# A graph network on one core: the convolutions' second parts one step later, and one scratch write fewer behind the gathers

## The chip, the cores and the metric

The kernel runs on one core of a Trainium2 chip. A core has five engines with queues of their own: TensorE multiplies matrices into PSUM, VectorE and ScalarE work element by element, GpSimd issues the gathers here, and SyncE issues plain transfers. The metric is the time of one execution on the device in microseconds. Three runs of the kernel before took 7125.32, 7131.07 and 7133.75 us; the median is 7131.07 us.

## The reference

There are 6250 nodes with 128 features and 200000 edges, sorted by destination. The function is a layer norm with a ReLU, two mesh convolutions with a group norm and a Silu behind each, and an attention over the edges; the parts are added up at the end. The change touches the convolutions only:

```python
def mesh_conv(x, src, dst, ea, w1, b1, g, bt, w2, b2):
    m = jnp.concatenate([x[dst], x[src], ea], axis=-1) @ w1 + b1
    m = jax.nn.silu(group_norm(m, g, bt))      # 8 groups of 16, per edge
    m = m @ w2 + b2
    out = jax.ops.segment_sum(m, dst, num_segments=n)
    cnt = jax.ops.segment_sum(jnp.ones((dst.shape[0],), m.dtype), dst, num_segments=n)
    return out / jnp.clip(cnt, 1.0)[:, None]
```

## The kernel before, in words

The edges are cut into 196 chunks of 1024 (`NCH` chunks, `NT` = 8 columns of 128 edges). A convolution multiplies by `w1` at the nodes and not at the edges: the part of the destination lies in the table `a_d`, the part of the source in `b_d`. Since the edges are sorted, a chunk needs a short run of 112 rows of `a_d`, which SyncE loads (L606), and a matmul with a one-hot matrix (`ohT`, made by ScalarE on L615 and L616 from loaded offsets) spreads them over the edges (L1000, tile `m`). The rows of `b_d` are gathered by GpSimd, eight indirect transfers of 128 rows to a chunk (`gather`, L622), into one of four buffers `g`. Behind a chunk's eight gathers GpSimd writes zeros into a scratch tile that nobody reads (L634), `REST` times: three times in the convolutions, four times in the attention. The next chunk's gathers stand behind these writes on GpSimd's queue.

A chunk's work in a convolution has two parts. The first part adds the gathered rows to `m` (L1006, VectorE, into one of four buffers `h`), squares the sum (L1008, ScalarE) and reduces it to one sum of squares for each edge and group (L1009, VectorE, tile `var`). Two chunks make a run: for a run ScalarE takes one square root (L1016, tile `sd`) and VectorE one reciprocal of it (L1093), into a PSUM tile that both chunks read. The second part makes the one-hot matrix of the destinations (L639), adds the sums of an earlier chunk to the node table (L1041), normalises with three VectorE passes (L1020, L1023, L1024), applies Silu (L1025, ScalarE), and sums over the edges by matmuls (L1030, TensorE, tile `u`). ScalarE then copies the sums of the chunk before out of PSUM, masked for two windows of 128 nodes (L1036).

`pipeline` writes all of this in steps. In step n a chunk two ahead is fetched (its loads and gathers are issued), the products of the next chunk are computed, the root of a run that is complete is taken (`root`), the one-hot offsets of the chunk two ahead are turned into ones and zeros, then come the second parts that fall due (`second`) and the first part of chunk n. `steps_of` says which second parts fall due in which step: those of a run are spread over the steps up to the end of the next run, and `lag` says how many steps behind the run's end they begin. In the kernel before, `lag` is 0 in the convolutions: in the step that takes the root, the run's first chunk has its second part, so chunk c has its second part in step c + 2. `in_order` pins the written order on VectorE, SyncE, ScalarE and TensorE; GpSimd's order follows from the gathers, each chunk behind the scratch writes of the chunk before.

From step 81 on, batches of four windows whose edges are all summed are processed as nodes between the steps (`conv_nodes`, 14 batches per convolution): a matmul with `w2`, the group norm, whose root is taken with that of a run, and the tables of the next stage. `plan_batches` finds from `steps_of` which chunks are done by then.

Of the kernel before, what the change touches and what calls it, by code (L numbers as in the profile page):

```python
# [24 lines left out]
HD = 16  # L25
NT = 8
CH = NT * P
REST = {1: 3, 2: 3, 3: 4}
G = 8
GC = 2  # L30
BN = 4
# [14 lines left out]
def kernel(ctx: ExitStack, tc: tile.TileContext, x, src, dst, eat, w, out):  # L46
# [280 lines left out]
    def spread(i):  # L327

        sizes, n = ([2, 4, 6], G) if i == 3 else ([1, 1], GC)
        rest, out = NCH, []  # L330
        while rest:
            out.insert(0, min(rest, sizes.pop(0) if sizes else n))
            rest -= out[0]
        return out

    def steps_of(i):


        ends, n, lag = {}, 0, int(i == 3)
        for m in spread(i):  # L340
            ends[n + m] = list(range(n, n + m))
            n += m
        waiting, todo = [], []
        for n in range(NCH + 1 + lag):
            waiting += ends.get(n - lag, ())
            steps = min([m + lag for m in ends if m + lag > n], default=n + 1) - n
            k = -(-len(waiting) // steps)
            todo.append(waiting[:k])
            waiting = waiting[k:]
        return ends, todo  # L350

    def plan_batches(i):

        ends, todo = steps_of(i)
        out, done = [], 0
        for n, now in enumerate(todo):
            done += len(now)
            if n % 8 == (4 if i == 3 else 1) and n > (40 if i == 3 else 80) and n + 6 < NCH \
                    and (i == 3 or n + 5 in ends):
                out.append((n, max(done - 3, 0)))  # L360
        return out if NWD else []
# [258 lines left out]
    def gather(k, g, table_d, rest=0):  # L620
        def start(t):
            return nc.gpsimd.indirect_dma_start(  # L622
                out=g[:, t, :table_d.shape[1]], out_offset=None, in_=table_d,
                in_offset=bass.IndirectOffsetOnAxis(ap=k.src[:, t:t + 1], axis=0))

        with ExitStack() as es:
            if rested and rest:
                es.enter_context(tc.issue_after(rested.pop().ins))
            for t in range(NT):
                last = start(t)  # L630
        if rest:
            with tc.issue_after(last.ins):
                for _ in range(rest):
                    last = nc.gpsimd.memset(nst2, 0.0)  # L634
                rested.append(last)

    def onehot(k, pools, iota):
        k.oh = pools["oh"].tile([P, NT, P], FP, name="oh")
        return nc.vector.tensor_tensor(  # L639
            k.oh, iota[:, None, :].to_broadcast([P, NT, P]),  # L640
            k.dm[:, :, None].to_broadcast([P, NT, P]), ALU.is_equal)
# [71 lines left out]
    def pipeline(i, stage, aside=iter(())):  # L713
# [5 lines left out]

        start = len(nc.cur_bb.bb.instructions)  # L720
        ends, todo = steps_of(i)
        starts = {n: j for j, (n, _) in enumerate(plans[i])}
        ahead = stage.ahead
# [240 lines left out]
    def conv(i):  # L964
# [4 lines left out]
        with ExitStack() as es:  # L969
# [49 lines left out]
            def normed(k):  # L1019
                nc.vector.tensor_tensor(  # L1020
                    k.mt.rearrange("p t (g c) -> p t g c", c=HD), k.mt.rearrange("p t (g c) -> p t g c", c=HD),
                    k.rs.rearrange("p (t g) -> p t g", g=H)[:, :, :, None].to_broadcast([P, NT, H, HD]), ALU.mult)
                nc.vector.tensor_tensor(k.mt, k.mt, over_edges(gam), ALU.mult)  # L1023
                nc.vector.tensor_tensor(k.mt, k.mt, over_edges(bet), ALU.add)  # L1024
                nc.scalar.activation(k.mt, k.mt, AF.Silu)  # L1025

            def summed(k):
                k.u = ps_.tile([P, PITCH], FP, name="u", tag="u", bufs=2)
                for t in range(NT):
                    nc.tensor.matmul(k.u[:, :wide], lhsT=k.oh[:, t, :], rhs=k.h[:, t, :wide],  # L1030
                                     start=(t == 0), stop=(t == NT - 1))

            def by_window(k):
                k.uw = up.tile([P, 2, PITCH], FP, name="uw")
                for q in range(2):
                    nc.scalar.activation(k.uw[:, q, :wide], k.u[:, :wide], AF.Copy,  # L1036
                                         scale=mask[:, q, k.c:k.c + 1])

            def add_late(k):
                s = U[:, bass.ds(value(w0_i, k.c, DVE, NW - 1), 2), :wide]  # L1040
                nc.vector.tensor_tensor(s, s, k.uw[:, :, :wide], ALU.add)  # L1041

            class Stage:
# [4 lines left out]
                def fetch(self, c):  # L1048
                    k = loads(c, pools, a_d[i], self.ahead)
                    k.g = gp.tile([P, NT, D], FP, name="g")  # L1050
                    gather(k, k.g, b_d[i], REST[i])
                    k.h = hs[c % len(hs)]
# [17 lines left out]
                        self.j = 0  # L1070

                def second(self, run, ks):
                    for n, k in enumerate(ks):


                        onehot(k, pools, iota)
                        if self.late:
                            add_late(self.late.pop(0))
                        if n == 0:
                            self.inverse(run)  # L1080
                        normed(k)
                        summed(k)
                        if self.sums:
                            by_window(self.sums[0])
                            self.late.append(self.sums.pop())
                        self.sums.append(k)
                    if not ks:
                        self.inverse(run)

                def inverse(self, run):  # L1090
                    if run:
# [68 lines left out]
    with ExitStack() as es:  # L1160
# [134 lines left out]
        class Stage:  # L1295
# [4 lines left out]
            def __init__(self, bp):  # L1300
                self.bp = bp
                self.runs = list(steps_of(3)[0].values())
                self.nb = load_runs(self.runs.pop(0), bp)

            def fetch(self, c):
                k = loads(c, pools, a_d[3], self.ahead)
                k.g = gp.tile([P, NT, KV], FP, name="g")
                gather(k, k.g, kv_d, REST[3])
                k.qe = []
# [142 lines left out]
```

## Time and profile before

| what | value |
| --- | --- |
| median of three runs | 7131.07 us |
| the profiled execution's own time | 7126.42 us |
| its span, first to last instruction | 7124.6 us |
| GpSimd busy | 5394.0 us (76%) |
| VectorE busy | 5144.2 us (72%) |
| TensorE matmuls busy | 3891.3 us (55%) |
| ScalarE busy | 3308.5 us (46%) |
| gathers of the convolutions | 3136, the first at 56.0 us, the last at 4615.8 us |
| gathers of the attention | 1568, from 4669.4 to 7050.1 us |
| granted TensorE clock, mean | 0.723 |

The span has three stages: the first convolution up to about 2300 us, the second up to about 4640 us, and the attention. In the lines of the profile, POOL is GpSimd, DVE is VectorE, ACT is ScalarE, PE is TensorE and SP is SyncE; `g<-b_d` means that tile `g` is written from `b_d`. A gather's row on POOL is the time in which GpSimd writes its transfer descriptors; the data lands later. Idle time that ended with nothing that the profile shows is called "issue".

### The profile page before, as it was taken

The numbers are of one execution on the slowest core, as the hardware profiler recorded it, in microseconds if no ns is written. First come the engines' busy times: TensorE is split into PE (matmuls) and PEld (weight loads), VectorE is DVE, ScalarE is ACT, GpSimd is POOL, SyncE is SP. The second block draws the span as 40 slices with busy tenths as digits, with TensorE's granted clock in tenths as the row PEclk, the third lists the DMA queues.
The fourth block names the chain that finished last, engine by engine and source line by source line (L and its number), as shares of the span: only waits on it lengthen the run. The fifth ranks groups of instructions, "written<-read, shape, count | busy, mean of one in ns | idle before, by whom it ended". The sixth has DMA issues, their size and how long they took to land. (4 is left out here: it accounts for less than half of the span.)

```text
span 7124.6 us, 74065 instructions
## 1 busy us (share of the span) xinstructions
PE 3891.3 (55%) x20957; PEld 3685.5 (52%) x20958; DVE 5144.2 (72%) x7564; ACT 3308.5 (46%) x5293; POOL 5394.0 (76%) x6678
## 2 busy tenths in 40 slices
PE   5555555555555455555555555545555555555555
PEld 4555555555555455555555555535555555555554
DVE  7777777777777576667777777736667777777778
ACT  5555555555555555555555555522223333333332
POOL 5777777777777677777777777767777777777774
PEclk7776677777777666666777777767777777777777
DMA  5433333333333333333333333344455555555553
GB/s 148 117 97 91 94 110 92 100 100 100 95 100 89 91 90 94 95 94 89 101 107 106 100 106 106 86 130 132 131 146 140 141 142 140 141 146 141 138 139 89
DMA packets 414321, 800.44 MB, mean 112 GB/s; under 512 B 101813, under 2 KB 274984, under 8 KB 379496
## 3 DMA queue, kind: packets, MB, share of 16 engines
q0 software_dynamic: 175616, 411.34, 22.2%
q1 hardware_dynamic: 232646, 380.69, 19.0%
q10 hardware_dynamic: 5632, 3.51, 0.2%
q8 instruction: 172, 2.82, 0.2%
q14 instruction: 255, 2.09, 0.1%
HBM read 754.19 MB, written 40.96 MB: 112 GB/s over the span
## 5 line engine op out<-in xcount | busy, mean ns | idle before, releaser
L622 POOL DMA_INDIRECT g<-b_d,src_i x3136 | 3000.7, 957 | 978.7 <-issue 940.0
L1030 PE MATMUL u<-h,oh 128*128 128x129 f32 (+1 forms) x6272 | 1395.6, 412 | 1891.2 <-ACT h L1025 1891.2
L1030 PEld LDWEIGHTS u<-h,oh 128*128 128x128 f32 x6272 | 1290.1, 314 | 1971.5 <-ACT h L1025 1963.9
L622 POOL DMA_INDIRECT g<-kv_d,src_i x1568 | 1532.4, 977 | 500.9 <-issue 468.8
L1251 PE MATMUL u<-v,oh 128*128 128x145 f32 x3136 | 750.0, 425 | 767.2 <-DVE nm L1284 765.6
L1251 PEld LDWEIGHTS u<-v,oh 128*128 128x128 f32 x3136 | 698.5, 308 | 801.9 <-issue 801.9
L1000 PE MATMUL m<-pk,ohT 117*128 117x128 f32 x6272 | 973.7, 321 | 134.9 <-DVE h L1006 101.1
L1006 DVE TENSOR_TENSOR h<-m,g 128x1024 f32<-128x1024 f32 x392 | 479.0, 1222 | 762.3 <-DMA g<-b_d,src_i 750.4
L1000 PEld LDWEIGHTS m<-pk,ohT 117*128 117x128 f32 x6272 | 942.0, 237 | 162.1 <-DVE h L1006 126.9
L1025 ACT ACTIVATE h<-h 128x1024 f32<-128x1024 f32 x392 | 414.2, 1057 | 1182.9 <-DVE h L1024 1182.9
L634 POOL MEMSET nst<- 128x392 f32 x1960 | 842.7, 430 | 79.3
L1008 ACT ACTIVATE sq<-h 128x1024 f32<-128x1024 f32 x392 | 413.9, 1056 | 653.8 <-DVE h L1006 650.8
L1009 DVE TENSOR_REDUCE var<-sq 128x64 f32<-128x1024 f32 x392 | 477.7, 1219 | 314.8 <-ACT sq L1008 312.2
L1187 DVE TENSOR_TENSOR g<-qe,g 128x384 f32<-128x384 f32 (+1 forms) x588 | 293.8, 511 | 549.7 <-DMA g<-kv_d,src_i 510.1
L615 ACT ACTIVATE ohT<-ohT,minus_p 112x1024 f32<-112x1024 f32 x588 | 669.9, 1139 | 16.2 <-DMA ohT<-rel_d 16.0
L616 ACT ACTIVATE ohT<-ohT 112x1024 f32<-112x1024 f32 x588 | 621.4, 1057 | 18.7
L1178 PE MATMUL qe<-pk,ohT 117*128 117x136 f32 x3136 | 512.8, 319 | 165.5 <-ACT ebs L1188 159.3
L1178 PEld LDWEIGHTS qe<-pk,ohT 117*128 117x128 f32 x3136 | 474.1, 225 | 198.8 <-ACT ebs L1188 192.3
L1023 DVE TENSOR_TENSOR h<-h,cps 128x1024 f32<-128x1024 f32 x392 | 478.4, 1220 | 13.5
L1024 DVE TENSOR_TENSOR h<-h,cps 128x1024 f32<-128x1024 f32 x392 | 478.4, 1220 | 13.4
L1020 DVE TENSOR_TENSOR h<-h,cps 128x1024 f32<-128x1024 f32 x392 | 475.3, 1212 | 5.9
L639 DVE TENSOR_TENSOR oh<-cps,dm 128x1024 f32<-128x1024 f32 x392 | 475.9, 1214 | 0.0
(265 smaller groups left out, 4383.9 us busy)
## 6 DMA issues: line engine op xcount, KB each, us to landing
ohT<-rel_d SPq DMA_DIRECT2D x294, 896.0 KB
g<-b_d,src_i POOLq DMA_INDIRECT x3136
pk<-a_d SPq DMA_DIRECT2D x588, 56.0 KB
g<-kv_d,src_i POOLq DMA_INDIRECT x1568
ohT<-in_eat_dram SPq DMA_DIRECT2D x294, 40.0 KB
a_d<-n_o SPq DMA_DIRECT2D x28, 256.0 KB
kv_d<-n_o SPq DMA_DIRECT2D x28, 256.0 KB
n_h<-h_d SPq DMA_DIRECT2D x19, 256.0 KB
```

Source lines behind the costliest of these rows:

```text
L615: nc.scalar.activation(k.ohT[:WN, :], k.ohT[:WN, :], AF.Square, bias=minus_p[:WN])
L616: nc.scalar.activation(k.ohT[:WN, :], k.ohT[:WN, :], AF.Relu, bias=1.0, scale=-4.0)
L622: return nc.gpsimd.indirect_dma_start(out=g[:, t, :table_d.shape[1]], out_offset=None, in_=table_d, in_offset=bass.IndirectOffsetOnAxis(ap ...
L634: last = nc.gpsimd.memset(nst2, 0.0)
L1000: nc.tensor.matmul(k.m[:, t, :], lhsT=lhs[:, t * P:(t + 1) * P], rhs=rhs, start=(j == 0), stop=(j == len(terms) - 1))
L1006: nc.vector.tensor_tensor(k.mt, k.m, k.g, ALU.add)
L1009: return lambda: nc.vector.tensor_reduce(var[:, j * NT * H:(j + 1) * NT * H], sq.rearrange("p t (g c) -> p (t g) c", c=HD), AX.X, ALU.add)
L1023: nc.vector.tensor_tensor(k.mt, k.mt, over_edges(gam), ALU.mult)
L1024: nc.vector.tensor_tensor(k.mt, k.mt, over_edges(bet), ALU.add)
L1030: nc.tensor.matmul(k.u[:, :wide], lhsT=k.oh[:, t, :], rhs=k.h[:, t, :wide], start=(t == 0), stop=(t == NT - 1))
L1178: nc.tensor.matmul(qe[:, t, :], lhsT=lhs[:, e], rhs=rhs, start=(j == 0), stop=(j == len(terms) - 1))
L1251: nc.tensor.matmul(k.u[:, :wide], lhsT=k.oh[:, t, :], rhs=k.v[:, t, :wide], start=(t == 0), stop=(t == NT - 1))
```

## The change

In the convolutions `lag` becomes 1: the second parts of a run begin in the step behind the one that takes its root, so chunk c has its second part in step c + 3. The reciprocal of a run's root is issued behind the second part of the step (which belongs to the run before and still reads the old reciprocals) and no longer between its one-hot matrix and its normalising passes. `REST` goes from 3 to 2 in both convolutions. The attention had `lag` 1 already and keeps its four writes. The lines below the edit move up by three (L1093 becomes L1090).

```diff
-REST = {1: 3, 2: 3, 3: 4}
+REST = {1: 2, 2: 2, 3: 4}
...
     def steps_of(i):
-        ends, n, lag = {}, 0, int(i == 3)
+        ends, n, lag = {}, 0, 1
...
                 def second(self, run, ks):
-                    for n, k in enumerate(ks):
+                    for k in ks:
                         onehot(k, pools, iota)
                         if self.late:
                             add_late(self.late.pop(0))
-                        if n == 0:
-                            self.inverse(run)
                         normed(k)
                         summed(k)
                         if self.sums:
                             by_window(self.sums[0])
                             self.late.append(self.sums.pop())
                         self.sums.append(k)
-                    if not ks:
-                        self.inverse(run)
+                    self.inverse(run)
```

## The prediction, made before the result was known

> **What bounds the kernel now.** I read the page's groups first. The chain that ended last goes back only to 7099 us, so it says nothing of the convolutions, and I went on with the list of waits and the timelines of GpSimd and VectorE.
>
> ```profile
> L622 POOL DMA_INDIRECT g<-b_d,src_i x3136 | 3000.7, 957 | 978.7 <-issue 940.0
> ...
> L1006 DVE TENSOR_TENSOR h<-m,g 128x1024 f32<-128x1024 f32 x392 | 479.0, 1222 | 762.3 <-DMA g<-b_d,src_i 750.4
> ...
> L634 POOL MEMSET nst<- 128x392 f32 x1960 | 842.7, 430 | 79.3
> ```
>
> Busy, mean ns, and behind the second bar the idle time before a group and what ended it. The gathers' engine is idle only for "issue": it waits for nobody. VectorE's first use of a gathered chunk (L1006) waits 750.4 us for gathers, over 392 chunks 1.91 us each.
>
> ```profile
> POOL g L622 <- issue: 1408.8, 4578, 2.1
> ...
> DVE h L1006 <- DMA g<-b_d,src_i: 750.4, 247, 15.7
> ...
> DVE cps L1093 <- ACT sd L1016: 98.8, 40, 4.2
> ```
>
> The waits: total, times, longest. The largest wait of VectorE is for the gathers. Its wait for the square root, which this change removes, is 98.8 us.
>
> ```profile
> 704.38 0.95 POOL L622 DMA_INDIRECT g<-b_d,src_i  x1 [0.28 <-DVE h L1024]
> ...
> 713.13 0.95 POOL L622 DMA_INDIRECT g<-b_d,src_i  x1 [0.30 <-issue]
> 714.08 1.41 POOL L634 MEMSET nst<- 128x392 f32 x3
> 715.76 0.95 POOL L622 DMA_INDIRECT g<-b_d,src_i  x1 [0.28 <-issue]
> ...
> 725.43 1.41 POOL L634 MEMSET nst<- 128x392 f32 x3
> 727.12 0.95 POOL L622 DMA_INDIRECT g<-b_d,src_i  x1 [0.27 <-issue]
> ```
>
> ```profile
> 704.29 1.22 DVE L1006 TENSOR_TENSOR h<-m,g 128x1024 f32<-128x1024 f32 x1 [0.15 <-DMA g<-b_d,src_i]
> ...
> 718.76 1.22 DVE L1006 TENSOR_TENSOR h<-m,g 128x1024 f32<-128x1024 f32 x1 [4.73 <-DMA g<-b_d,src_i]
> ...
> 727.35 1.22 DVE L1006 TENSOR_TENSOR h<-m,g 128x1024 f32<-128x1024 f32 x1
> ...
> 742.39 1.22 DVE L1006 TENSOR_TENSOR h<-m,g 128x1024 f32<-128x1024 f32 x1 [5.05 <-DMA g<-b_d,src_i]
> ```
>
> GpSimd's chunks start at 704.38, 715.76 and 727.12: a period of 11.37 us made of eight gathers 1.25 apart, three scratch writes in 1.41, and gaps. VectorE takes 14.47 - 4.73 = 9.74 us of its own for the step with a reciprocal and 8.59 for the one without, 9.2 on average. So GpSimd sets the pace of both convolutions, and the scratch writes are part of the pace.
>
> **The change, part by part.**
>
> 1. One scratch write fewer per convolution chunk, 392 in all. Three take 1.41 us from start to end, so one is 0.47 (0.43 busy and a gap). The groups say the same: 842.7 + 79.3 us over 1960 is 0.47. The next chunk's first gather is queued right behind and nothing else on that queue: 11.37 becomes 10.90. The last chunk's writes of each convolution are on nobody's path, so 390 x 0.47 = 183 us, taken off as long as GpSimd stays last.
>
> 2. The second part (one-hot, add of the window sums, three normalising passes, ScalarE's Silu, TensorE's sums) moves one step back. Nothing is added or removed in the steady state; it issues no DMA, and its load of the window's number into VectorE's register moves along. On ScalarE the Silu keeps its place, behind the root and the two one-hot passes of L615 and L616, and in a root step its input is ready a reciprocal (0.96 us) sooner. In a step with a root, VectorE now puts the reciprocal behind the normalising passes of an older chunk, some 3.7 us (3 x 1.25) later than before, so ScalarE's square root (0.40 us behind a 1.28 table load) has time: the 98.8 us of waits go. VectorE is not last, so this is worth nothing directly; it is added to its slack: 1.91 - 0.47 + 0.25 = 1.69 us per chunk remain. Where the node batches run (1600 to 2200 us) the gather wait is 70.2 us over 52 steps (600 us at 11.5), 1.35, and the root's wait 36.2, 0.70: 1.35 - 0.47 + 0.70 = 1.58 remain. Were the root's wait to reappear elsewhere in full, 0.88 would. What is late next is the gather, as now.
>
> 3. A chunk's h is held a step longer. The four h buffers now make L1006 of a chunk wait for the sums of the chunk four back, which TensorE did in the step just before:
>
> ```profile
> 2011.26 1.22 DVE L1024 TENSOR_TENSOR h<-h,cps 128x1024 f32<-128x1024 f32 x1
> ...
> 2012.51 1.06 ACT L1025 ACTIVATE h<-h 128x1024 f32<-128x1024 f32 x1 [1.36 <-DVE h L1024]
> ...
> 2013.62 3.81 PE L1030 MATMUL u<-h,oh 128*128 128x129 f32 x16 [6.98 <-ACT h L1025]
> ...
> 2021.30 1.22 DVE L1006 TENSOR_TENSOR h<-m,g 128x1024 f32<-128x1024 f32 x1
> ```
>
> The sums end at 2017.43 and the next L1006 starts at 2021.30, 3.9 us later, in a step where VectorE did not wait for a gather at all. Cost nothing; the cover is VectorE's own step. Were it gone, each step would lose what TensorE is late, after VectorE's 1.6 us of slack. The sums took 2.4 to 3.8 us in this trace, so they would have to take over 9 us (3.8 + 3.9 + 1.6). Lower bound: no gain, since nothing waits for h sooner.
>
> 4. SyncE's queue keeps its order: row loads, one-hot loads and node stores are issued where they were. GpSimd's queue keeps its order but for the writes. The node batches' windows come from one chunk earlier; worked out from the destinations, they are 14 per convolution still and the last one still reaches window 40 of 40, so no mending loop runs.
>
> 5. The ends. The last chunk's second part now has another chunk's before it, after the last gather has landed: from 4625.19 to 4630.89 one takes 5.70 us with its reciprocal (0.59), so 5.1 more. One step earlier a doubled step (two chunks' second parts, 10.2 us) now stands before the last chunk's L1006, where VectorE waited only 0.77 us, and that may push it by 0 to 3 us: I take 1. About 6 us per convolution, 12 in all (bounds 8 and 17).
>
> Sum: -183 + 12 = -171. The profiled execution took 7126.4 us (its span is 7124.6) and the median of the runs is 4.7 above it: 7126.4 - 171 = 6955, and 6960 on the scale of the median.
>
> **A rule that speaks against it.** Gathers that start beside VectorE's L1041 (flat and uw, both in SBUF, 0.42 us) still took 0.94: one ran from 2003.41 while L1041 ran from 2003.98. The Trainium skill ("SBUF — State Buffer", "Who interferes with whom") says that GpSimd shares a port pair with VectorE and that a VectorE instruction with two SBUF inputs contends with GpSimd work that reads SBUF, whichever is issued first. If by that rule every chunk lost one L1041 to it, 392 x 0.42 = 165 us would be given back and the sum be 7125. The page itself infers that descriptor generation is spared, and the row agrees, so I keep the sum by the row.
>
> **Rivals.**
>
> A. VectorE becomes last where node batches run. For it: some root steps there have 13.35 us between two L1006 (1999.04 to 2012.39), with 3.35 of wait for the root. Against: the 1.58 us left above. If the stretches with batches (about half of the steps) gained nothing, 92 of the 183 us go: 7052.
>
> B. GpSimd isn't paced by its writes after all; the gathers go earlier but the data lands no sooner, say behind the one-hot loads. For it: chunks land unevenly, the one that ended issuing at 714.08 was waited for until 718.7 (4.6 us), the one that ended at 725.43 was there by 727.35 (under 1.9). Against: a late landing doesn't hold up the next issue, and every second chunk lands early. No gain, only the ends: 7143.
>
> C, slower: gathers stretch once less rest lies between them. For it: at the start gathers took 1.29, 1.23, 1.56, 1.93 and 2.62 us (55.95 to 66 us) beside VectorE's long preparation, so they can. Price: it decides from 0.47 us more per chunk on. With one gather in eight at the middle one of these, 1.56, a chunk takes 0.62 more and 0.47 less: 392 x 0.15 = 59, and 12 for the ends: 7131 + 71 = 7202. Against: the median of 3136 gathers is 0.944 and whatever lies beside them in the steady loop has hardly moved it.
>
> **How the numbers follow.** Full gain 0.72, its own range 6930 (the ends cost nothing and some of the gathers' stalls go too) to 7000; A 0.08; B 0.06; C 0.14. A measurement tells a change from none at about 0.2%, 14 us, so 7117 to 7145 is the same. B falls in it, with the ends on its upper edge, so I give 0.05 to the same and 0.01 to slower. Faster 0.80, same 0.05, slower 0.15. The range from 6930 to 7145 holds the first case but for its edges, A and most of B, and leaves out C.
>
> **What would show it.** Right: 1568 scratch writes instead of 1960; GpSimd's chunk period 10.9 us with idle time still "issue"; VectorE still waits for gathers, some 600 to 680 us at L1006; its wait for sd under 15 us; hardly any wait of L1006 for TensorE's u. Wrong: L1006 without gather waits and instead waits on u or sq (A); the period 10.9 at GpSimd's queue but with waits on VectorE's buffers (A); gathers with a mean clearly above 957 ns (C); the period at 11.4 in spite of two writes (B, C). The step most likely to fail is the first: that 0.47 us off GpSimd's queue arrives whole.

## The result, and the profile after

The changed kernel takes 6950.44 us (median of four runs, 6949.85 to 6952.75) against 7130.9 us for the kernel before beside it (median of four, 7125.32 to 7133.75). The ratio is 0.9748, with a 95% interval from 0.9732 to 0.9765. The profiled execution's span goes from 7124.6 to 6948.8 us, 175.8 less.

The same groups in the page of the changed kernel (busy, mean ns, then the idle time before them and what ended it):

```profile
L622 POOL DMA_INDIRECT g<-b_d,src_i x3136 | 2997.9, 956 | 981.1 <-issue 940.2
...
L1006 DVE TENSOR_TENSOR h<-m,g 128x1024 f32<-128x1024 f32 x392 | 478.1, 1220 | 658.8 <-DMA g<-b_d,src_i 637.0
...
L634 POOL MEMSET nst<- 128x392 f32 x1568 | 676.2, 431 | 56.8
```

There are 392 scratch writes fewer, a gather takes what it took (956 ns, before 957), and GpSimd's idle time before the gathers is still "issue". VectorE still waits for gathers, 637.0 us instead of 750.4. Its list of waits in the changed kernel (total, times, longest):

```profile
DVE h L1006 <- DMA g<-b_d,src_i: 637.0, 220, 10.8
...
DVE h L1006 <- PE u L1030: 6.4, 2, 3.2
...
DVE cps L1090 <- ACT sd L1016: 1.6, 3, 0.6
```

The wait of the reciprocal for the root has gone from 98.8 to 1.6 us, and the longer life of `h` costs 6.4 us in two places. GpSimd's timeline of the changed kernel:

```profile
707.97 0.92 POOL L634 MEMSET nst<- 128x392 f32 x2
709.16 0.95 POOL L622 DMA_INDIRECT g<-b_d,src_i  x1 [0.27 <-issue]
...
718.85 0.92 POOL L634 MEMSET nst<- 128x392 f32 x2
720.04 0.95 POOL L622 DMA_INDIRECT g<-b_d,src_i  x1 [0.28 <-issue]
```

The next chunk's gathers begin 10.88 us after those of this one, where it was 11.37.

The starts of the gathers divide the gain by stages:

| stretch | before, us | after, us | difference |
| --- | --- | --- | --- |
| first convolution, first gather of its first chunk to first gather of its last | 2251.9 | 2153.7 | -98.2 |
| from there to the second convolution's first gather | 60.0 | 64.7 | +4.7 |
| second convolution, the same | 2239.2 | 2147.7 | -91.5 |
| last convolution gather to the attention's first | 53.64 | 59.66 | +6.0 |
| attention's first gather to the end | 2455.2 | 2458.7 | +3.5 |

With 0.35 us less before the first gather these make the 175.8, but for rounding. The gain lies evenly over both convolutions, 0.50 and 0.47 us per chunk. In neither trace does GpSimd wait for VectorE in the steady loop, so the later second part had nothing there to release.

### The profile page after: what moved, and what is told of

The parts are those of the page before. It is cut to its first block, busy times and chain, and to the rows that moved or that the text cites. A ratio compares the mean times of both kernels' runs of the same rounds, so it can differ in the third digit from the quotient of the medians.

```text
span 6948.8 us, 73672 instructions
## 1 busy us (share of the span) xinstructions
PE 3858.2 (56%) x20957; PEld 3651.1 (53%) x20958; DVE 5141.9 (74%) x7564; ACT 3306.9 (48%) x5293; POOL 5225.6 (75%) x6286
## 5 line engine op out<-in xcount | busy, mean ns | idle before, releaser
L1030 PE MATMUL u<-h,oh 128*128 128x129 f32 (+1 forms) x6272 | 1348.8, 402 | 1682.0 <-ACT h L1025 1682.0
L1030 PEld LDWEIGHTS u<-h,oh 128*128 128x128 f32 x6272 | 1246.4, 304 | 1763.0 <-ACT h L1025 1758.3
L1248 PE MATMUL u<-v,oh 128*128 128x145 f32 x3136 | 765.7, 432 | 771.6 <-DVE nm L1281 768.9
L1000 PE MATMUL m<-pk,ohT 117*128 117x128 f32 x6272 | 973.0, 321 | 218.6 <-DVE h L1006 174.9
L1000 PEld LDWEIGHTS m<-pk,ohT 117*128 117x128 f32 x6272 | 937.6, 237 | 248.8 <-DVE h L1006 198.1
L1006 DVE TENSOR_TENSOR h<-m,g 128x1024 f32<-128x1024 f32 x392 | 478.1, 1220 | 658.8 <-DMA g<-b_d,src_i 637.0
L634 POOL MEMSET nst<- 128x392 f32 x1568 | 676.2, 431 | 56.8
```

Source lines behind the costliest of these rows:

```text
L1000: nc.tensor.matmul(k.m[:, t, :], lhsT=lhs[:, t * P:(t + 1) * P], rhs=rhs, start=(j == 0), stop=(j == len(terms) - 1))
L1006: nc.vector.tensor_tensor(k.mt, k.m, k.g, ALU.add)
L1248: nc.tensor.matmul(k.u[:, :wide], lhsT=k.oh[:, t, :], rhs=k.v[:, t, :wide], start=(t == 0), stop=(t == NT - 1))
```

## The experiments

The theory is the prediction's: GpSimd sets the pace, the write removed gives the whole gain, and the later second part gives nothing itself. The rivals are that the gain comes from the later second part (the root's wait), and that fewer writes stretch something else.

On the three chips that ran the experiments the kernel before takes 7439 to 7470 us and not 7131, so every ratio below is against the kernel before on the same chip, and no time is set against the first comparison without saying so. The first four experiments shared one chip, the next four a second, the last four a third. None of the kernels leaves out or changes a part of the computation; the scratch writes carry nothing.

### One part at a time, and no writes at all

The write alone, with the second parts where they were:

```diff
-REST = {1: 3, 2: 3, 3: 4}
+REST = {1: 2, 2: 2, 3: 4}
```

> The kernel before with two scratch writes per convolution chunk; lag stays 0. Theory (GpSimd's queue paces the convolutions and a write costs 0.47 us of it): 7131 - 183 = 6948 us, without the cost at the ends, so at most 12 us below the changed kernel. Rival (the later second parts are what lets the shorter period be used, since VectorE with its waits for the root needs up to 10 us per chunk in the batch stretches and more in single steps): the batch stretches gain nothing and it takes 7030 to 7060 us. In both, the wait for sd stays near or above 99 us.

The second part one step later alone (on the changed kernel):

```diff
-REST = {1: 2, 2: 2, 3: 4}
+REST = {1: 3, 2: 3, 3: 4}
```

> The changed kernel with three scratch writes again; only the second parts come one step later. Theory: nothing in the steady state, since VectorE is not last, and 6 to 12 us more at the ends of the two convolutions: 7137 to 7143 us, with the wait for sd gone and VectorE's wait for gathers up by about as much. Rival (the root's wait is on the path): 7131 - 99 = 7032 us.

No scratch write in the convolutions, once with the later second part and once on the kernel before:

```diff
-REST = {1: 2, 2: 2, 3: 4}
+REST = {1: 0, 2: 0, 3: 4}
```

> The changed kernel with no scratch writes in the convolutions; the attention keeps four. Theory: GpSimd's period falls by two more writes, 2 x 0.47 x 390 = 367 us, to about 9.97 us (eight gathers 1.25 apart) plus some 0.1 of stalls, still above the 9.4 to 9.5 us that VectorE takes by itself: 6950 - 367 = 6583, up to 6640 if VectorE is last in some stretches. Rival (gathers stretch or the data lands later once nothing lies between the chunks): above 6700 us with a mean gather clearly over 957 ns, or VectorE's gather waits growing.

```diff
-REST = {1: 3, 2: 3, 3: 4}
+REST = {1: 0, 2: 0, 3: 4}
```

> The kernel before with no scratch writes in the convolutions, lag 0. Here VectorE's own time per chunk with its waits for the root (9.4 without batches, up to 10.0 with them) is as large as GpSimd's 9.97. Theory: where batches run VectorE is last in part, so the later second parts begin to pay: 6583 to 6680 us, and slower than the kernel without writes and with lag 1 by 10 to 60 us. Rival (lag never matters): equal to it or 6 to 12 us faster.

The kernel before took 7438.64 us here.

| kernel | median, us | ratio to before [95%] |
| --- | --- | --- |
| the write alone | 7663.6 | 1.0279 [1.0243, 1.0315] |
| the later second part alone | 7359.3 | 0.9882 [0.9857, 0.9907] |
| no writes, later second part | 7526.7 | 1.0113 [1.0089, 1.0137] |
| no writes, second part where it was | 8260.77 | 1.1093 [1.1061, 1.1125] |

All four expectations were missed. Here the write removed costs 2.8%, and the step that was to be worth nothing gains 1.2%. That is either a rival come true or another condition of the chip; the changed kernel itself on such a chip is the next thing to run.

### The changed kernel, and the parts again, on a second chip

The changed kernel unaltered, and three of the kernels above with the same edits:

> The changed kernel itself, beside the runs of the parts, since the first four runs came from a chip on which the kernel before took 7439 us and TensorE had slow episodes (16 matmuls in up to 17 us instead of 3.8), which the trace of before doesn't have. If the chip has these episodes again: theory that they end some 2 to 3 us after GpSimd's gathers pause: two writes pause less than three, so it is slower than the lag alone (7359) and, being spread over fewer late engines, faster than two writes without lag (7664): 7400 to 7500 us. If the chip has none: 6950 us.

> Two writes, lag 0, a second time. On a chip without the slow episodes (before near 7131 us): 6938 to 6950 us, by the theory that GpSimd's queue paces; rival (lag is needed to use the shorter period) 7030 to 7060. On a chip with them: 7664 us again, about 1.028 of before.

> Three writes, lag 1, a second time. Without the slow episodes: 7134 to 7143 us, nothing gained in the steady state; rival (the root's wait is on the path) 7032. With them: 7359 us again, about 0.988 of before.

> No writes in the convolutions, lag 1, a second time. Without the slow episodes: 6583 to 6640 us, the fastest of all. With them: 7527 us again, slower than before, with GpSimd at 9.97 us per chunk waiting for VectorE's buffers.

| kernel | median, us | ratio to before [95%] |
| --- | --- | --- |
| the changed kernel | 7427.03 | 0.9944 [0.9922, 0.9966] |
| the write alone | 7688.86 | 1.0278 [1.0219, 1.0337] |
| the later second part alone | 7369.35 | 0.9885 [0.9846, 0.9925] |
| no writes, later second part | 7534.42 | 1.0095 [1.0066, 1.0125] |

All four came out as expected for a chip in this condition, and the two chips agree on the parts. The whole change gains 0.6% here, not 2.5%: with the later second part in place, taking the write away costs 57.7 us (7427.03 against 7369.35).

### Where the time goes on these chips

To have the kernel before in a trace on such a chip, it was run unaltered on the third:

> The kernel before, for its trace on a chip of these experiments. If this chip gives some 7440 to 7470 us: TensorE has slow episodes here (groups of 16 matmuls over 5 us, waits of TensorE put down to issue of several hundred us), of which the trace of before that the prediction read has none (its longest group takes 3.81 us). If it gives 7131: no such group.

It took 7464.79 us, the median there being 7468.44. Its list of waits (total, times, longest):

```profile
PE u L1030 <- issue: 585.3, 438, 10.4
...
PE m L1000 <- issue: 523.9, 740, 8.7
POOL g L622 <- DVE h L1006: 290.8, 66, 12.0
DVE cps L1093 <- ACT sd L1016: 153.0, 29, 13.9
...
DVE h L1006 <- DMA g<-b_d,src_i: 54.1, 15, 14.8
```

In the first comparison's trace GpSimd never waited for VectorE in the steady loop, and VectorE waited 750.4 us for gathers. Here that wait is 54.1, and GpSimd stands 290.8 us waiting for a `g` buffer: the pace is no longer GpSimd's alone. What is new is TensorE's idle time between the matmuls of one chunk, ended by nothing that the profile shows. Inside the groups of 16 matmuls at L1000 and L1030 it adds up to 692.8 us here and to 0.0 in both traces of the first comparison. (The rows "<- issue" alone would not prove it: on these chips part of the semaphore events are missing in the traces, and waits before a group fall under "issue" too.) The timeline of TensorE and GpSimd in the changed kernel on the second chip shows such a stretch:

```profile
1817.57 0.94 PE L1000 MATMUL m<-pk,ohT 117*128 117x128 f32 x7
...
1818.71 0.27 PE L1000 MATMUL m<-pk,ohT 117*128 117x128 f32 x1 [0.20 <-issue]
...
1819.43 0.36 PE L1000 MATMUL m<-pk,ohT 117*128 117x128 f32 x1 [0.45 <-issue]
...
1820.84 0.27 PE L1000 MATMUL m<-pk,ohT 117*128 117x128 f32 x1 [1.05 <-issue]
...
1822.27 0.27 PE L1000 MATMUL m<-pk,ohT 117*128 117x128 f32 x1 [1.16 <-issue]
...
1823.24 0.94 POOL L622 DMA_INDIRECT g<-b_d,src_i  x1 [0.30 <-issue]
1823.67 0.37 PE L1000 MATMUL m<-pk,ohT 117*128 117x128 f32 x1 [1.13 <-issue]
...
1824.17 0.93 POOL L634 MEMSET nst<- 128x392 f32 x2
1824.40 0.37 PE L1000 MATMUL m<-pk,ohT 117*128 117x128 f32 x1 [0.35 <-issue]
...
1825.80 0.37 PE L1000 MATMUL m<-pk,ohT 117*128 117x128 f32 x1 [1.03 <-issue]
...
1826.51 0.79 PE L1000 MATMUL m<-pk,ohT 117*128 117x128 f32 x2 [0.34 <-issue]
```

Seven matmuls pass in 0.94 us, and then each single one starts 0.7 or 1.4 us after the one before it, though the profile shows no semaphore that it waits for; the weight loads, not shown, start at the same spacing in between. GpSimd's last gather ends at 1824.18, and from 1826.5 on TensorE runs at its pace again. I call such a stretch an episode; in others two to four matmuls pass together between two of the long steps. A group of 16 matmuls takes up to 28 us (the write alone, second chip); without episodes no group of 16, at L1000 or L1030, takes over 3.81 us in either kernel. Counted over the 784 groups of the convolutions (392 at each line, from the first start to the last end; steps of 0.6 us and more inside groups that lie less than 3 us apart make one episode):

| kernel | writes | second part | groups over 5 us | longest episode, us |
| --- | --- | --- | --- | --- |
| before, first comparison | 3 | as before | 0 | none |
| changed, first comparison | 2 | later | 0 | none |
| before, third chip | 3 | as before | 191 | 92.5 |
| the write alone, first chip | 2 | as before | 139 | 41.6 |
| the later second part alone, second chip | 3 | later | 182 | 79 |
| changed kernel, second chip | 2 | later | 144 | 25.5 |
| no writes, later second part, first chip | 0 | later | 131 | 15.5 |
| no writes, first chip | 0 | as before | 105 | 22.8 |

The ends of the episodes point to what they hang on. From the beginning of the last pause in the gathers to the end of an episode it is 2.2 us in the median in the kernel before, 2.1 with the later second part alone, 2.6 in the changed kernel (where 95 of 120 episodes end 2 to 3 us after a pause begins), and 2.6 with the write alone. Without writes the only pauses are those in which GpSimd waits for a buffer; there it is 3.0 us with the later second part and 4.1 without it. In the kernel with no writes and the second part where it was, the timeline has this:

```profile
723.15 0.94 POOL L622 DMA_INDIRECT g<-b_d,src_i  x1 [0.30 <-issue]
...
725.52 0.38 PE L1030 MATMUL u<-h,oh 128*128 128x129 f32 x1 [1.72 <-issue]
...
727.65 1.91 PE L1030 MATMUL u<-h,oh 128*128 128x129 f32 x5 [0.35 <-issue]
```

The next gather there waits until 737.96 for VectorE (13.87 us), which waits for TensorE, which is slowed until the gathers stop. Such waits of GpSimd add up to 1621.1 us in this kernel, 1330 more than in the kernel before (third chip); less the writes' 390 x 3 x 0.48 = 562 us that leaves 768 of the 822 us lost. The attention, with four writes, has no episode: no group of 16 matmuls at its sums takes over 4.21 us, and from its first gather to the end it takes 2462 to 2473 us on these chips.

### Is it the length of the pause, or its place?

Three writes make a pause of 1.7 us, in which an episode often does not end. Three kernels vary the pause at the later second part, all on the third chip. One write each behind the third, sixth and eighth gather:

```diff
-        if rest:
-            with tc.issue_after(last.ins):
-                for _ in range(rest):
-                    last = nc.gpsimd.memset(nst2, 0.0)
+            for _ in range({3: {2: 1, 5: 1, 7: 1}, 4: {7: 4}}.get(rest, {}).get(t, 0)):
+                with tc.issue_after(last.ins):
+                    prev = nc.gpsimd.memset(nst2, 0.0)
```

> Three writes and lag 1, but one write behind the third, the sixth and the eighth gather of a chunk, so GpSimd's period stays 11.37 us and its longest pause falls from 1.7 us to about 0.75. Theory (a slow episode of TensorE ends only when the gathers pause for some 2 us): episodes get longer and it is slower than the lag alone with the writes together (7359 to 7369 us): 7450 to 7700. Rival (only GpSimd's pace counts): 7359 to 7369.

Six writes behind every second chunk and none behind the others, which costs GpSimd the same as three:

```diff
-                    gather(k, k.g, b_d[i], REST[i])
+                    gather(k, k.g, b_d[i], 6 * (c % 2))
```

> Lag 1 with six writes behind every second chunk's gathers and none behind the others: the same mean period of 11.37 us, a pause of 3.1 us every 22.7. Theory (pauses end episodes): no episode lasts much over 23 us, where those with three writes behind each chunk reached 79; the time lies within 100 us of 7369 on either side, since fewer pauses come but each is long enough. Rival (only the pace counts): 7359 to 7369, and episodes of any length.

Four writes behind every chunk, as the attention has:

```diff
-REST = {1: 2, 2: 2, 3: 4}
+REST = {1: 4, 2: 4, 3: 4}
```

> Lag 1 with four writes: a pause of 2.2 us behind each chunk and a period of 11.84. Theory (pauses end episodes): almost every episode ends in the pause it meets first; without any late chunk it takes 7139 + 183 = 7322 us, with some 7330 to 7400, as fast as three writes or a little faster, and then the fastest here. Rival (only the pace counts): 7369 + 100 to 183 = 7470 to 7550.

The kernel before took 7468.44 us on this chip.

| kernel | median, us | ratio to before [95%] | groups over 5 us | longest episode, us |
| --- | --- | --- | --- | --- |
| three writes, split | 7439.21 | 0.9959 [0.9935, 0.9984] | 125 | 44.2 |
| six behind every second chunk | 7462.19 | 0.9996 [0.9976, 1.0016] | 139 | 18.2 |
| four behind every chunk | 7324.06 | 0.9813 [0.9772, 0.9854] | 0 | none |

The split writes miss their expectation (7450 to 7700), and the run is not the comparison that it was meant to be. A write between two gathers lengthens the gap there from 0.30 to 0.61 us only, so three of them cost GpSimd 0.93 us and not 1.4: where it does not wait, its chunk takes 10.90 us, which is the period of two writes together (10.88) and not of three (11.37). Against the changed kernel (7427.03 on the second chip) they are 12 us slower, and episodes did not get longer. The short pauses end episodes too: 59 of 107 end 2 to 3 us after one begins, where an even spread over the 4.05 us between them would give a quarter. So neither a long pause nor its place behind the chunk is shown to be needed for that. Six writes behind every second chunk let no episode last longer than two chunks, as expected, but new ones begin in the long stretch between the pauses, and nothing is gained. With four writes there is no episode, and the time is just below the expected 7330 to 7400, at the 7322 given for a kernel without any late chunk. GpSimd's timeline in that kernel:

```profile
703.46 1.88 POOL L634 MEMSET nst<- 128x392 f32 x4
705.63 0.95 POOL L622 DMA_INDIRECT g<-b_d,src_i  x1 [0.29 <-issue]
...
715.32 1.89 POOL L634 MEMSET nst<- 128x392 f32 x4
717.49 0.95 POOL L622 DMA_INDIRECT g<-b_d,src_i  x1 [0.28 <-issue]
```

Its waits (total, times, longest) are again those of a kernel that GpSimd paces:

```profile
POOL g L622 <- issue: 1431.0, 4652, 2.1
...
DVE h L1006 <- DMA g<-b_d,src_i: 975.5, 301, 15.7
```

The pause is 2.2 us, the period 11.86, and the time is what GpSimd alone makes of it. It beats the kernel before by 1.9% on this chip and is the fastest of all on these chips, the changed kernel (7427.03 on the second) included. Whether the longer pause or the longer period keeps episodes away is not shown, since the two came together, and four writes ran on one of the chips only. Where there are no episodes it would be behind the changed kernel, by the writes it adds: its two convolution stretches take 368.9 us more than the changed kernel's in the first comparison, with 780 writes more, which is 0.473 us for each.

## Why the prediction was right, point by point

The forecast was 6960 us and the time is 6950.44, in the likeliest case's own range. The sum was -171 and the span shows -175.8.

**Step 1**, 390 writes of 0.47 us, -183: right in place and size. GpSimd's period went from 11.37 to 10.88, idle before the gathers is still "issue", and the two convolutions' stretches give -98.2 and -91.5. That is 6.7 more than the step said, and it lies in the first convolution (half of 183 is 91.5). The traces divide it: in that stretch the gathers' own rows add up to 4.5 us less than before (1501.2 and 1496.7 us), since fewer of them are stretched; in the second convolution they are 2.1 us longer. Without this both stretches gain 93.6 us, so a write is worth 0.48 us and not 0.47. The four-write kernel gives nearly the same price from the other side, 0.473 us for each write over 780.

**Step 2**, the later second part worth nothing itself, the root's wait gone: right as to the wait (98.8 to 1.6 us) and as to VectorE, which still waits 637.0 us for gathers, 1.63 us for a chunk; the estimate was 1.69. That this part is worth nothing could not be run under the conditions of the first comparison. It is worked out only, and across chips: 7324.06 for four writes without episodes, less 390 x 0.48 = 187, is 7137 for three, about 6 above the kernel before; the attention alone, which neither part touches, takes 7.0 us longer on that chip than in the changed kernel's trace.

**Step 3**, four `h` buffers held a step longer, nothing: right, 6.4 us of waits in two places.

**Step 4**, the order of the queues: GpSimd's timeline shows chunk, writes, chunk as before, with two writes. The attention after it takes 3.5 us more from its first gather to the end, which was not in the sum.

**Step 5**, the ends, +12: the two crossings measured +4.7 and +6.0, together 10.7.

**The rule** on shared ports would have given back 165 us for 7125. The prediction set it aside by a row in which the gather began first (2003.41, and L1041 at 2003.98), and that row can't show it. Where L1041 begins first, the gather is held. In the kernel before:

```profile
3004.13 0.41 DVE L1041 TENSOR_TENSOR flat<-flat,uw 128x256 f32 x1
3004.19 1.18 POOL L622 DMA_INDIRECT g<-b_d,src_i  x1 [0.30 <-issue]
...
3005.67 0.94 POOL L622 DMA_INDIRECT g<-b_d,src_i  x1 [0.30 <-issue]
```

Gathers that begin 0.03 us or more behind an L1041, with over 0.15 us of it still to run, take longer than the usual 0.944 us by that rest less 0.128 us, to within 7 ns in all 76 such cases of the kernel before and 79 of the changed kernel. So the reason that the prediction gave is wrong, and the gathers are blocked. That the forecast did not suffer is luck: only 149 of the 3136 gathers begin during an L1041 (126 in the changed kernel), and together they lose 8.0 us before and 10.6 us after, not 165.

**Rival A** (VectorE last where batches run) falls: from the 81st chunk on, where the batches run, the gathers gain 0.51 us for a chunk in the first convolution and 0.46 in the second, against 0.50 and 0.48 up to there. **Rival B** (GpSimd not paced by its writes) falls by the period. **Rival C** (less rest stretches the gathers) falls in the first comparison. On the three other chips its sign is right for the write, and its mechanism is not: gathers stay at 953 to 958 ns in the mean, and it is TensorE that slows while gathers run. There **step 1 fails**: GpSimd's queue is 0.48 us shorter for a chunk, but GpSimd then waits for a buffer, and the write removed costs 57.7 us at the later second part and 219 to 225 at the earlier one. On the second chip:

```profile
POOL g L622 <- DVE h L1006: 432.9, 142, 6.2
...
POOL g L622 <- DVE h L1006: 184.2, 68, 6.2
```

The first line is the changed kernel, the second the later second part alone. The wait grows by 248.7 us and the writes take off 390 x 0.48 = 187, which leaves 62 us against the 57.7 measured. With the write alone the wait is 676.7 us, 386 more than in the kernel before (290.8, third chip), and 386 - 187 = 199 stands against the 219 measured. **Step 2 fails** there too: the later second part alone gains 79 to 100 us, and its wait is 107 us shorter than in the kernel before. Why it is shorter is open. **Step 3** does not hold there either: in the changed kernel on the second chip VectorE stands 904 us before L1006, and 827 us of that end with a semaphore that TensorE counts up (the profile calls it "remote", without an instruction); whether it is for the products or for an `h` buffer the trace does not tell.

## What to carry to other kernels

Where one queue paces a loop and its idle time is "issue", an instruction taken off that queue is worth its pitch times its count, and this held within 4% here over 390 and over 780 instructions as long as no episode came. But a filler that does nothing may be there as a pause: before it goes, look in the trace at whether any other engine has gaps that no semaphore explains, and time the change on more than one chip, because one comparison here showed -2.5% and another -0.6% for the same kernels. Where such gaps exist, one filler more can beat one fewer.

## What the runs showed of the hardware that was not expected

On three chips, and not in the first comparison, TensorE fell into episodes in which its matmuls start singly or a few together, 0.7, 1.4 or 2.1 us apart and now and then 2.8 or 3.5, with nothing in the profile to wait for. No such step begins later than 3.8 us behind the end of a gather; in the kernels with writes behind every chunk the median episode ends 2.1 to 2.6 us after the gathers pause. With pauses of 1.7 us in each 11.4 us 191 of 784 groups were hit, with 2.2 us in each 11.9 none (at the later second part; with 1.7 us there, 182).

A gather whose descriptors GpSimd begins to write while VectorE adds two SBUF tiles (L1041) is held until that addition ends: up to 1.21 us instead of 0.94. One that begins before it is not.

It is not the clock. The Trainium skill ("TensorE: Matmul & The Clock Gate", "Part 1: The HAM clock gate") describes a gate that passes half of the pulses when the array has been idle and all of them when it is busy. The traces agree with two clocks, 0.5 and 1.0, and a group of 16 at the lower takes 3.8 us; in an episode the recorded clock is one of these two, a single matmul in the rows above still shows 0.27 to 0.37 us, and yet a group takes up to 28 us.

Nor has a transfer become slow as far as they were looked at: the gathers' packets of 4096 bytes keep their median of 211 to 220 ns, and the fetches of instructions take 0.9 to 2.3 us in the traces with and without episodes. The same Trainium skill says of the memory's ports ("SBUF — State Buffer", "Who interferes with whom") that TensorE waits for nobody; in these runs it stands still while gathers run, and at what they don't show, so whether a port is involved stays open. Also open is why the first comparison had none. Whether two writes without the later second part give about 6948 us where there are no episodes couldn't be tried, since all three chips of the experiments had them.
